# Row length of the involution stage's loads and stores: whole rows of 3136 to 6272 bytes, or runs of at most 896 bytes

## Chip, cores and metric

One core of one Trainium2 chip. The time is the device time of one execution in microseconds (us). A core has five engines that run their own instruction lists side by side: PE (TensorE, the matrix unit; its weight loads are listed apart as PEld), DVE (VectorE), ACT (ScalarE), POOL (GpSimd) and SP (SyncE, which here only issues DMA transfers). Sixteen DMA engines move data between the device memory (DRAM) and the on-chip memory, whose tiles have 128 partitions.

## The reference

A batch of 8 images of 256 channels, 56 x 56 pixels, float32, goes through two layers. `gn` is a group normalization over 32 groups, without scale and shift.

```python
# layer 0: involution, 16 groups of 16 channels, 7 x 7 neighbourhood
h = gn(x)
ker = einsum('bchw,oc->bohw', h, w_reduce) + b_reduce      # 256 -> 64 channels
ker = einsum('bchw,oc->bohw', ker, w_span) + b_span        # 64 -> 49 * 16
patches = the 49 shifted copies of h, zero outside the image
x = x + (ker * patches).sum(over the 49)                   # one kernel for the 16 channels of a group
# layer 1: residual block with ternary 3 x 3 convolutions
h = gn(x)
y1 = relu(batch_norm(tri_conv(h, w1)))
y2 = batch_norm(tri_conv(y1, w2))
x = x + relu(y1 + y2)
```

`tri_conv` quantizes its weights to -1, 0 and 1, convolves, and adds the product with the centre tap once more. `batch_norm` takes its mean and variance over the whole batch.

## The kernel before

The program has four stages, one after the other: the involution (layer 0), the first convolution, the second convolution, and a last pass that normalizes, adds and writes the output. The edited lines belong to the involution alone.

**Tiling of the involution.** The 256 channels are cut into 4 quarters of 64. A tile `x` of an image and a quarter (`xs[b, c]`) holds the 64 channels twice in its 128 partitions: the upper half of the image in the first 64, the lower half in the others, 28 x 56 = 1568 pixels (6272 bytes) in each partition. A half image is cut into patches of 3 x 8 pixels: 10 rows of patches (`ty`), 7 patches (`k`) in a row. With the border of a 7 x 7 neighbourhood a patch has 9 x 14 = 126 input pixels.

**The work for a row of patches.** The involution of a patch is a matrix product: the patch's 126 input pixels stand in the partitions of a tile `q`, and a generated matrix `a` maps them to the output pixels. `q` is a neighbourhood load (`load_q`, L726): 128 partitions of 7 patches x 128 channels, 896 floats or 3584 bytes each, from a copy of the image that lies ready in that order in DRAM. There are 8 images x 4 quarters x 10 rows = 320 of them. For each row:

- PE multiplies (`apply_row`, L839): 7 patches x 2 halves x 4 channel groups = 56 small matmuls into the accumulator tile `pa`;
- ACT and DVE take the result out (`pick_out`, L860: ACT at L867, DVE at L868), and POOL adds it to the image tile (L871);
- POOL adds the normalization's constants to a later `q` (`fill_rim`, L746, operation at L752), ACT writes the lower border (`fill_end`, L761).

**Beside it** PE generates the matrix `a` of the next quarter (`generate`, L804: products of the reduced image `kr` with the span weights `wl` into `pg`, taken to `a` by ACT at L827 and DVE at L831), reduces the next image (`reduce`, L700, products `pk`) and multiplies the kernel sums (`constant`, L774, products `ks`). DVE takes the statistics of the next image (`gn1_stats`), and quantizes the convolution weights in pieces (`quantize`, L277): a piece of 576 bytes a partition is loaded (L289), six planes are made, and they are stored in rows of 192 bytes (L318).

**Transfers and their order.** All of them go through SP's queue, in the order of the text. For each row of patches: a store of a finished image tile (`store_x1`, L891, rows 2 and 3 of the next quarter: 64 channels x 1568 floats, for the upper and the lower half) or half a tile of the next image (`load_x`, L599: 128 partitions x 784 floats, 3136 bytes), then one neighbourhood load (`prefetch`, L877), then the pieces of the quantization. SP waits at each until its buffer is free, and the ones after it wait behind it. There are 5 buffers for `q`, so the load for row n + 5 is issued when PE has read row n; POOL's rim addition for row n + 3 stands in row n (`surround`, `PLEAD = 2`). There are 7 buffers for `x`; a tile's buffer comes free when its two stores have landed.

**What fixes the order.** The text is recorded in order, and `pin` ties each engine's instructions to it; no scheduler moves anything. At the start SP issues the 8 halves of the first image, the weights `wf` for the first quantization, two tiles of span weights and biases (`sums`, L945 and L946), and the first five neighbourhood loads. The later stages load rows of 6496 bytes (`raw`), store rows of 6272 (`y1d`, `y2d`), and the last stage moves rows of 12,544.

Of the kernel before, what the change touches and what calls it, by code (L numbers as in the profile page):

```python
# [17 lines left out]
P = 128  # L18
# [10 lines left out]
CH = P // 2  # L29
# [6 lines left out]
PY, PX = 3, 8  # L36
# [4 lines left out]
QY, QX = PY + K - 1, PX + K - 1  # L41
# [6 lines left out]
HQ = TY * PY + K - 1  # L48
# [7 lines left out]
NQB = 5  # L56
PLEAD = 2
RIM_AT = 1

NCB = 4  # L60
NC = NHW // NCB
# [22 lines left out]
def involution_tri_block_kernel(  # L84
# [3 lines left out]
    nc = tc.nc  # L88
# [484 lines left out]
    with ExitStack() as ph1:  # L573
# [25 lines left out]
        def load_x(b, c, j):  # L599

            if j == 0:
                xs[b, c] = xpool.tile([P, NHW], F32, tag="x", name=f"x_{b}_{c}")
            part = slice(j * NHW // 2, (j + 1) * NHW // 2)
            nc.sync.dma_start(xs[b, c][:, part], x[b, c, :, part])

        def gn1_stats(b, c, j):

# [56 lines left out]
        prm, xs = {}, {}  # L664
        for c in range(NCQ):
            for j in range(2):
                load_x(0, c, j)
# [58 lines left out]
        def load_q(b, c, ty):  # L726

            q = qpool.tile([P, TX, P], F32, tag="q", name=f"q_{b}_{c}_{ty}")
            nc.sync.dma_start(q.rearrange("p k c -> p (k c)"),
                              x_nb[b, c, (HQ - QY - PY * ty) * QX:(HQ - QY - PY * ty) * QX + P, :])  # L730
            return q

        def rim_of(b, c):

            sides = work.tile([P, 2, P], F32, tag="sides", name=f"sides_{b}_{c}")
            tops = work.tile([P, 3, CH], F32, tag="tops", name=f"tops_{b}_{c}")
            rim = prm[b][3][:, c]
            for dst, k0, k1, f1 in ((sides, 0, 2, P), (tops, 2, 5, CH)):
                shape = [NQ, k1 - k0, f1]
                nc.gpsimd.tensor_tensor(dst[:NQ], rims_sb[:NQ, k0:k1].unsqueeze(2).to_broadcast(shape),  # L740
                                        rim[:NQ, :f1].unsqueeze(1).to_broadcast(shape), ALU.mult)
            low = work.tile([P, CH], F32, tag="low", name=f"low_{b}_{c}")
            nc.gpsimd.tensor_copy(low[:NQ], rim[:NQ, CH:])
            around[b, c] = sides, tops, low
# [132 lines left out]
        def prefetch():  # L877
            if queue:
                k = queue.pop(0)
                loads[k] = load_q(*k)  # L880
                bare.append(k)

        def surround(keep=PLEAD):
            for k in filled:
                fill_end(*k)
            filled.clear()
            while len(bare) > keep or bare and not queue:
                filled.append(bare.pop(0))
                fill_rim(*filled[-1])

        def store_x1(b, c, h):  # L891
            nc.sync.dma_start(
                x1_d[b][c // 2][c % 2 * CH:(c % 2 + 1) * CH, h * NHW:(h + 1) * NHW],
                xs[b, c][h * CH:(h + 1) * CH])

        gst = {}

# [91 lines left out]
        for m, (b, c) in enumerate(quarters):  # L989
# [6 lines left out]
            for ty in range(TY):  # L996
                r = c * TY + ty

                if last is not None and ty in (2, 3):
                    store_x1(*last, ty - 2)  # L1000
                elif more and r in X_AT:
                    load_x(b + 1, X_AT.index(r) // 2, X_AT.index(r) % 2)
                row = apply_row(b, c, a, ty)
                prefetch()

                if r == PARAMS_AT:
                    norm = params(b + 1) if more else gn2_params(0, b)
                next(norm, None)

                if ty == 1 and last is not None:  # L1010
                    gn2_stats(*last, TY)
                elif ty >= 2:
                    gn2_stats(b, c, ty - 1)
                if more and 4 <= r < 20:
                    gn1_stats(b + 1, (r - 4) // NCB, (r - 4) % NCB)
                pick_out(b, c, ty, *row)
                surround()
                if ty == RIM_AT and m + 1 < len(quarters):
                    rim_of(*quarters[m + 1])
                next(norm, None)  # L1020
                for _ in range(PER_ROW[ty]):
                    next(gen, None)
                if m * TY + ty >= QUANT_AT:
                    next(quant, None)
                pin()
# [6 lines left out]
        for h in range(2):  # L1032
            store_x1(*last, h)
# [46 lines left out]
    with ExitStack() as ph4:  # L1080
# [10 lines left out]
        for j in range(B * CT):  # L1091
            b, t = j // CT, j % CT
# [97 lines left out]
```

## Time and profile before

| what | value |
|---|---|
| median of 4 runs | 2215.27 us (2213.56 to 2220.21) |
| the profiled execution, device time | 2213.51 us |
| its span, first to last instruction | 2211.7 us |
| mean granted PE clock | 0.906 of full speed |
| involution, about 0 to 1090 us | PE busy 84% from 60 to 1085 us |
| two convolutions, 1100 to 1980 us | PE busy 98%, 440 us each |
| last pass, 1980 to 2212 us | DMA engines busy 99% |
| DMA packets in all | 156,252; 440.11 MB |
| neighbourhood load | 320 times 448 KB; issue on SP 0.33 us, landed after 4.2 us (medians) |
| image load | 64 times 392 KB; landed after 5.0 us |
| x1 store | 64 times 392 KB; landed after 5.5 us |

How to read the profile: *busy* is the time in which an engine had an instruction in work. A *wait* line names the waiting instruction, what released it, the sum of the idle time before it, how often, and the longest. "issue" there means that nothing the profile shows released it. The *DMA share* is the mean busy share of the sixteen DMA engines; queue q1 is the one that SP issues to, q8 carries packets of the kind "instruction". A DMA *packet* is one row of one transfer; each engine closes its part of a transfer with a packet of 4 bytes. The *granted clock* is the share of the full clock that PE was allowed. The *chain* of waits is followed back from the last instruction to what released each step.

### The profile page before, as it was taken

The page shows a single profiled execution, that of the slowest core. Times are in us where ns is not written, and L with a number is a line of the kernel's source. Part 1 is how long each engine was busy: PE and PEld are TensorE (multiplying, and loading weights), DVE is VectorE, ACT ScalarE, POOL GpSimd, SP SyncE. Part 2 cuts the span into 40 slices and gives each one's busy share as a digit, 9 for nine tenths or more (in the row PEclk, how much of TensorE's full clock was granted, in tenths as well). Part 3 has the DMA queues.
Part 4 walks back from the last instruction along what each step waited for, and adds up shares of the span by engine and source line. Part 5 has one row for each costly group of instructions (what it writes and reads, how often), then busy time and mean ns, then how long its engine had stood idle before and what let it go on. Part 6 is the DMA issues. An engine that isn't in the chain of part 4 may idle for free.

```text
span 2211.7 us, 71625 instructions
## 1 busy us (share of the span) xinstructions
PE 1756.4 (79%) x30192; PEld 1613.6 (73%) x30192; DVE 1731.5 (78%) x3257; ACT 1425.3 (64%) x3505; POOL 589.7 (27%) x965
## 2 busy tenths in 40 slices
PE   4888787988879788798599999997999999970000
PEld 3777676767767676677599999997999999970000
DVE  5768869677696867855599999998999999984444
ACT  3867677776767667677556666665566666663434
POOL 1546546564564646556500000000000000000000
PEclk9989899999999989899799999998999999985555
DMA  5558658575675757656643333335233333369999
GB/s 180 188 161 258 198 171 262 178 251 186 213 232 158 234 168 245 208 171 200 230 167 119 119 119 119 133 133 206 90 119 119 119 119 130 134 255 410 430 428 398
DMA packets 156252, 440.11 MB, mean 199 GB/s; under 512 B 63774, under 2 KB 74012, under 8 KB 148508
## 3 DMA queue, kind: packets, MB, share of 16 engines
q1 hardware_dynamic: 150336, 405.50, 53.0%
q10 hardware_dynamic: 5596, 30.03, 3.3%
q8 instruction: 239, 3.92, 0.7%
q14 instruction: 81, 0.66, 0.1%
HBM read 323.28 MB, written 112.20 MB: 197 GB/s over the span
## 4 chain that ended last, share of the span: by engine, by line
PE 63%; DMA 11%; DVE 9%; issue 8%; POOL 5%; ACT 3%; SPq 0%; ACTq 0%; POOLq 0%; DVEq 0%
PE c L516 39%; PE pg L823 11%; PE pa L854 7%; PE pk L711 4%; DMA y1f<-y1d 4%; POOL q L752 2%; ACT a L827 2%; DMA out_y<-x1f 2%; POOL x L871 2%; PE ks L787 1%; DMA x1f<-x1d 1%; DVE x1f L1103 1%; POOL x L801 1%; DMA y2f<-y2d 1%; DVE a L831 1%
## 5 line engine op out<-in xcount | busy, mean ns | idle before, releaser
L516 PE MATMUL c<-pl,wq 128*128 128x392 f32 x4608 | 857.4, 348 | 14.1 <-ACT pl L386 14.1
L516 PEld LDWEIGHTS c<-pl,wq 128*128 128x128 f32 x4608 | 855.5, 190 | 15.8 <-ACT pl L386 14.5
L827 ACT ACTIVATE a<-pg,bt 126x126 f32<-126x126 f32 (+1 forms) x2048 | 530.8, 456 | 112.4 <-PE pg L823 110.8
L823 PE MATMUL pg<-kr,wl 64*126 64x140 f32 (+1 forms) x6144 | 466.7, 297 | 59.3 <-issue 25.7
L823 PEld LDWEIGHTS pg<-kr,wl 64*126 64x126 f32 x6144 | 406.0, 199 | 85.4 <-issue 31.3
L854 PE MATMUL pa<-a,q 126*32 126x48 f32 x17920 | 288.9, 213 | 107.6 <-issue 83.7
L854 PEld LDWEIGHTS pa<-a,q 126*32 126x32 f32 x17920 | 237.3, 115 | 184.9 <-issue 113.4
L831 DVE TENSOR_TENSOR a<-pg,bt 126x504 f32<-126x504 f32 (+4 forms) x640 | 281.6, 482 | 53.4 <-PE pg L823 51.4
L868 DVE SCALAR_TENSOR_TENSOR inv<-pa,gn1s,inv 128x168 f32<-128x168 f32 x320 | 118.4, 370 | 220.2 <-ACT inv L867 219.0
L871 POOL TENSOR_TENSOR x<-x,inv 128x168 f32<-128x168 f32 x320 | 166.3, 520 | 461.8 <-DVE inv L868 399.4
L386 ACT CAST pl<-r 128x812 fp32r<-128x812 f32 x192 | 162.5, 868 | 143.2 <-DVE r L381 123.7
L366 POOL MEMSET xp<- 128x116 f32 x32 | 6.2, 195 | 825.6 <-DVE a L381 825.6
L752 POOL TENSOR_TENSOR q<-q,sides 126x256 f32<-126x256 f32 (+1 forms) x320 | 224.5, 702 | 4.2 <-DMA q<-in_x_nb 4.2
L387 DVE TENSOR_TENSOR pl<-r,pl 128x812 fp32r<-128x812 f32 x192 | 187.1, 1002 | 27.4 <-ACT pl L386 26.2
L451 ACT ACTIVATE dummy<-y,nc 128x1568 f32<-128x1568 f32 (+1 forms) x128 | 200.2, 1564 | 4.8 <-DVE y L536 3.5
L867 ACT ACTIVATE inv<-pa,gn1s 128x168 f32<-128x168 f32 x320 | 133.3, 417 | 102.2 <-PE pa L854 77.3
L143 DVE BATCH_NORM_STATS2 st<-x 128x6 f32<-128x392 f32 x256 | 138.0, 555 | 12.0 <-DMA x<-in_x 9.4
L801 POOL TENSOR_TENSOR x<-x,add 128x504 f32<-128x504 f32 (+1 forms) x128 | 126.7, 1021 | 12.2 <-ACT add L795 12.2
L1050 ACT ACTIVATE xp<-raw,gn 128x392 f32<-128x392 f32 (+1 forms) x124 | 82.5, 721 | 59.6 <-DVE a L381 58.8
L1070 ACT ACTIVATE xp<-raw,bi_bn,sc_bn 128x392 f32<-128x392 f32 (+1 forms) x124 | 82.3, 720 | 58.8 <-DVE a L381 57.1
L1101 DVE SCALAR_TENSOR_TENSOR y1f<-y2f,sc_bn,y1f 128x3136 f32<-128x3136 f32 (+2 forms) x20 | 56.6, 2831 | 63.9 <-DMA y2f<-y2d 50.1
L1103 DVE TENSOR_TENSOR x1f<-x1f,y1f 128x3136 f32<-128x3136 f32 (+2 forms) x20 | 55.3, 2772 | 50.9 <-DMA out_y<-x1f 31.5
(174 smaller groups left out, 1794.5 us busy)
## 6 DMA issues: line engine op xcount, KB each, us to landing
q<-in_x_nb SPq DMA_DIRECT2D x320, 448.0 KB, 4.2
raw<-x1d SPq DMA_DIRECT2D x32, 812.0 KB, 5.9
raw<-y1d SPq DMA_DIRECT2D x32, 812.0 KB, 5.8
x<-in_x SPq DMA_DIRECT2D x64, 392.0 KB, 5.0
x1d<-x SPq DMA_DIRECT2D x64, 392.0 KB, 5.5
y1d<-y SPq DMA_DIRECT2D x30, 784.0 KB, 3.3
y2d<-y SPq DMA_DIRECT2D x30, 784.0 KB, 3.3
y1f<-y1d SPq DMA_DIRECT2D x14, 1568.0 KB, 14.4
```

The source lines that it names most:

```text
L143: nc.vector.bn_stats(st[:, j, :], xt[:, j * NC:(j + 1) * NC])
L386: nc.scalar.copy(hi, r)
L387: nc.vector.tensor_tensor(lo, r, hi.bitcast(F32), ALU.subtract)
L451: nc.scalar.activation(dst, v, f, bias=shift[:, to:to + 1], accum_out=stats[:, to, j, n:n + 1])
L516: nc.tensor.matmul(ps[:, to, :NM], wq[k][:, t, dx, to * P:(to + 1) * P], part[:, t, :, dx:dx + W], start=(c == 0), stop=(c == last))
L752: nc.gpsimd.tensor_tensor(v, v, z, ALU.add)
L801: nc.gpsimd.tensor_tensor(x_, x_, v, ALU.add)
L823: nc.tensor.matmul(dst, wl[rows, c, gp, o:o + NQ], kr[py][rows, px, :], start=True, stop=True)
L827: nc.scalar.activation(dst[:, g + 1, p0 + j], ps[1][:NQ, j * nt + t0:j * nt + t1], AF.Identity, bias=bt[:, c, g + 1, p0 + j:p0 + j + 1])
L831: nc.vector.tensor_tensor(dst[:, g, p0:p0 + n].rearrange("q p t -> q t p"), ps[0][:NQ, t0 * n:t1 * n].rearrange("q (t p) -> q t p", p=n), ...
L854: nc.tensor.matmul(ps[o:o + 32, k * 2 * n:(k + 1) * 2 * n], q[:NQ, k, o:o + 32], av[:, t + k, g * 2 * n:(g + 1) * 2 * n], start=True, stop ...
L871: nc.gpsimd.tensor_tensor(xv, xv, iv.rearrange("p t (y x) -> p y t x", x=PX), ALU.add)
```

## The change

Three transfers of the involution are given a longest run: the image loads (`load_x`), the neighbourhood loads (`load_q`) and the stores of the involution's result (`store_x1`). The argument limits the last dimension of the transfer's access pattern, in bytes; the builder cuts a row into equal pieces that fit. The bytes moved, their places, the order of the instructions on every engine and all computation stay. A neighbourhood row of 3584 bytes becomes 4 runs of 896, an image row of 3136 bytes 4 runs of 784, a store's row of 6272 bytes 7 runs of 896.

```diff
 PLEAD = 2
 RIM_AT = 1
+RUN = 896
...
             part = slice(j * NHW // 2, (j + 1) * NHW // 2)
-            nc.sync.dma_start(xs[b, c][:, part], x[b, c, :, part])
+            nc.sync.dma_start(xs[b, c][:, part], x[b, c, :, part], max_dma_last_dim=RUN)
...
             q = qpool.tile([P, TX, P], F32, tag="q", name=f"q_{b}_{c}_{ty}")
             nc.sync.dma_start(q.rearrange("p k c -> p (k c)"),
-                              x_nb[b, c, (HQ - QY - PY * ty) * QX:(HQ - QY - PY * ty) * QX + P, :])
+                              x_nb[b, c, (HQ - QY - PY * ty) * QX:(HQ - QY - PY * ty) * QX + P, :],
+                              max_dma_last_dim=RUN)
             return q
...
         def store_x1(b, c, h):
             nc.sync.dma_start(
                 x1_d[b][c // 2][c % 2 * CH:(c % 2 + 1) * CH, h * NHW:(h + 1) * NHW],
-                xs[b, c][h * CH:(h + 1) * CH])
+                xs[b, c][h * CH:(h + 1) * CH], max_dma_last_dim=RUN)
```

## The prediction

> **What bounds the kernel now.** I read first the table of stretches, cut at the program's stages (columns: stretch, its length, busy time of PE, PE's weight loads, DVE, ACT and POOL with instruction counts, granted clock, mean busy share of the 16 DMA engines, GB/s).
>
> ```profile
> 60.00:1085.00 1025.00, 864.27 (x25044) 729.07 (x25040) 742.36 (x2041) 738.87 (x2619) 569.82 (x909) 0.93 0.66 206
> 1100.00:1540.00 440.00, 429.48 (x2308) 428.38 (x2308) 418.61 (x542) 279.81 (x379) 3.12 (x16) 0.98 0.37 138
> 1980.00:2211.70 231.70, 0.00 (x0) 0.00 (x0) 113.06 (x51) 91.11 (x39) 0.00 (x0) 0.50 0.99 416
> ```
>
> All three edited transfers run in the involution, the first row. There PE is busy 84% and every other engine less, the DMA engines 66%: PE sets the pace, with 161 us of idle. The convolutions are PE alone, the last stage is DMA alone, and neither issues an edited transfer. So the question is what the edit does to those 161 us and to the first 60. Second, the waits of PE in that stretch (us, times, longest):
>
> ```profile
> PE pa L854 <- issue: 76.5, 57, 3.8
> PE pg L823 <- issue: 25.7, 25, 3.2
> PE pg L823 <- DVE a L831: 21.1, 12, 3.4
> PE pa L854 <- ACT a L827: 13.0, 16, 1.7
> ```
>
> 102.2 us in 82 waits have no releaser among the instructions. Third, the DMA queues in the same stretch:
>
> ```profile
> q1 hardware_dynamic: 119181, 207.79, 64.7%
> q8 instruction: 198, 3.24, 1.3%
> q<-in_x_nb SPq DMA_DIRECT2D x315, 448.0 KB, 4.2
> ```
>
> q8 carries 198 packets of 16 KB, and PE ran 25,044 + 25,040 instructions: 253 for each packet, so I read q8 as PE's program, fetched over the same DMA engines; a packet took 0.013 x 16 x 1025 / 198 = 1.08 us. Fourth, one of the waits, in the timeline of PE:
>
> ```profile
> 242.21 0.74 PE L854 MATMUL pa<-a,q 126*32 126x48 f32 x49
> 246.72 0.38 PE L854 MATMUL pa<-a,q 126*32 126x48 f32 x7 [3.78 <-issue]
> ```
>
> PE stops after 49 of a row's 56 matmuls, all from one tile pair, so no data is awaited. The stretches around it:
>
> ```profile
> 242.90:244.30 1.40, 0.05 (x5) 0.00 (x0) 1.40 (x6) 1.39 (x6) 0.27 (x1) 1.00 1.02 355
> 244.30:245.20 0.90, 0.00 (x0) 0.00 (x0) 0.90 (x3) 0.00 (x0) 0.90 (x2) 1.00 0.99 346
> 245.20:246.70 1.50, 0.00 (x0) 0.00 (x0) 0.95 (x5) 0.00 (x0) 0.05 (x1) 0.58 0.42 107
> ```
>
> From 242.9 to 246.8 q8 has one packet, and a look at 244.20 to 244.35 holds its start. PE had run out 1.3 us before, while all engines worked on SP's data; the packet took about 1 us, and PE went on 1.5 us after it. So **the program fetch queues behind the data loads, and that is PE's largest idle in this stage.** In the convolutions PE has no issue wait: the DMA share is 0.37 and a fetch lasts over 20 us (37 in 885).
>
> **The change part by part.** The built program has the same instructions in the same order on all five engines; only shapes differ: a neighbourhood load of 128x896 words becomes 128x4x224, an image load 128x784 becomes 128x4x196, an x1 store 64x1568 becomes 64x7x224. So the limit is in bytes, and rows are 896, 784 and 896 bytes. Each of 16 engines had 8, 8 and 4 rows of a transfer and gets 32, 32 and 28: 24 more in each case.
>
> *Price of a row.* The last stage, on 12,544-byte rows above all, moves 422 GB/s, 26.4 bytes per ns and engine. The other end is a stretch that is nearly all 192-byte rows (the quantized weights' store), 1.2 us long:
>
> ```profile
> DMA packets 803, 0.18 MB, mean 147 GB/s; under 512 B 795, under 2 KB 795, under 8 KB 803
> q1 hardware_dynamic: 803, 0.18, 66.6%
> ```
>
> 0.666 x 16 x 1.2 = 12.8 us, less 8 rows of 3584 bytes at 0.136, leaves 11.7 us; over 768 rows (the other 27 small packets are 4-byte closings) that is 15 ns, of which 192 / 26.4 = 7.3 are the bytes: 7.7 ns of each row are fixed. 24 more rows: 0.185 us per transfer and engine. A neighbourhood load goes from 8 x 143.5 = 1.15 to 32 x 41.6 = 1.33 us (+16%). From 328.5 to 329.1 us, 128 rows of 576 bytes took 41.1% of 16 x 0.6 us, 30 ns each; the formula gives 29.5. The low bound is no fixed part, +0; the high one is the 12.8/803 = 16 ns of a whole small packet for each added row, 0.38 us. I take 0.185, the value that fits three sizes. The Trainium skill (DMA: Bandwidth & Descriptors, Specifications) puts line rate at 512 bytes and up, by which this edit would cost nothing on the engines; the 576-byte rows here run at 19 of 26.4 bytes per ns, so the row decides.
>
> The stretch from 60 to 1085 us has 315 neighbourhood loads, 55 image loads and 62 stores: 432 x 0.185 = 80 us more on every engine, and its share goes from 0.66 to 0.74.
>
> *The start.* Between 8 and 28 us the DMA share is 0.98 to 1.05, and the chain of waits goes through the load of the span weights, issued 13.8 and landed 24.7, behind eight image loads on SP's queue. Added: 8 x 0.185 = 1.5 us, bounds 0 and 3.0 (8 x 0.38). The neighbourhood loads there stand behind it.
>
> *Landing of the neighbourhood loads.* They land in 4.2 us (median); with 0.185 and one queued neighbour's 0.185 more it is 4.6. SP's issue also grows: 0.33 us now, 0.55 for the three-dimensional weight store, 0.2 more. Cover: a load is asked for two rows (2 x 1025/315 = 6.5 us) ahead of its rim addition on POOL, and that is about three rows ahead of PE's use. POOL waited for a load 6 times, 5.9 us in all. If all of those grow by 0.6 it is 4 us on POOL, which waits 392 us for DVE anyway; I put 2 us on the path (bounds 0 and 8). What is late next is SP: it stands for 573 us before neighbourhood loads until PE frees a buffer, 130 us before weight pieces until a weight store has landed, 16 us before image loads until an x1 store has. Each of these 55 landing waits grows by some 0.2 to 0.4 us and holds the neighbourhood load behind it, within the same two rows. Without that cover, 315 x 0.4 = 126 us.
>
> *The program fetch.* No row shows how its wait depends on row size, so it is bounded. Straight line: 102.2 us over 198 fetches is 0.52 us each at share 0.66, and none at 0.37: 1.8 us per unit of share, times 0.08, times 198: +28 us. Queue: with a wait that goes as share/(1 - share), 1.94 becomes 2.85 (x1.47): +48 us. High: the engine that carries the fetches has 198 x 1.08 / 1025 = 0.21 more, 0.87 becoming 0.95; the same law would triple its wait, but a PE that waits also asks for less, so I stop at a doubling, +102 us. Low: a fetch that only waits for a fixed number of accepted rows waits less, as each is 41.6 instead of 143.5 ns; half of the idle in that proportion, -36 us. I take +48: the wait shown above lasted ten row times of SP's queue after PE had stopped, nearest to a backlog, and the backlog grows.
>
> The same skill page (Queues, rings and completion order) says that a DMA engine goes round its queues packet by packet, some 9 to 17 descriptors each, at most 64. By that rule a fetch waits for one packet only: 17 rows of 41.6 ns, 0.7 us, instead of a load's 8 rows, 1.15 us, and 198 x 0.45 = 89 us at most would be gained; with whole loads of 32 rows as packets it is 198 x 0.18 = 36 us lost. It speaks against my sign; the wait above, of at least 1.3 us, is longer than one packet by either reading.
>
> **Sum.** The profiled execution took 2213.51 us (span 2211.7). 2213.5 + 1.5 + 2 + 48 = 2265. The median of the runs shown, 2215.3, is 1.8 above it: **2267 us**, +2.3%.
>
> **Rivals.**
> - *Faster: the fetch slips between small rows.* Place: q8 against SP's queue; it decides if the rows accepted ahead of a fetch are limited in number. For it: the row in service is 3.4 times shorter. Against: the convolutions' rows are nearly twice as long and their fetches stall nothing, and the wait shown was ten rows. 2213.5 + 3.5 - 36 + 1.8 = 2183.
> - *Hidden.* Fetches are as late as before and PE's cover takes the rest: 2213.5 + 3.5 + 1.8 = 2219 (+0.16%). For it: an average of 0.74 leaves 26% free. Against: the stalls come where the share is 1 already.
> - *The loads become the bound.* If rows in bursts cost more (a load alone from 138.1 to 139.9 us took 75% of 16 x 1.8 us, 167 ns a row, 1.2 of 0.14), the fetching engine's 0.95 passes 1: 1025 x 0.95 x 1.2 = 1169, +144: 2213.5 + 3.5 + 144 + 1.8 = 2363.
> - *The edit does nothing* if rows were counted in words; the built shapes exclude it.
>
> **How the numbers follow.** Forecast (2235 to 2335) 0.63; loads as bound 0.06; hidden 0.12; faster 0.19. Faster than by 0.2% (4.4 us, about what a measurement can tell): 0.19; within: 0.12; slower: 0.69. The range must take in the hidden case and part of the faster one: 2200 to 2335, with 0.12 below and 0.08 above; the high end is 2213.5 + 3 + 8 + 102 + 1.8 = 2328 and some clock loss (after the wait above the granted clock was 0.58).
>
> **What would show it.** Right: under 2 KB some 170,000 more packets, q1's share in the involution near 0.72, PE's issue waits near 150 us, POOL's waits for loads under 12 us, the convolutions and the last stage as long as now to 2 us. Wrong: issue waits below 102 us (the faster rival), or unchanged (hidden); POOL or PE waiting for loads for over 40 us (loads as bound); a row of 896 bytes that takes over 55 or under 36 ns.

## The result and the profile after

| | median | lowest to highest | runs |
|---|---|---|---|
| before | 2213.92 us | 2204.68 to 2235.29 | 72 |
| after | 2225.53 us | 2212.29 to 2236.01 | 48 |

After / before, compared within the groups of runs that shared a chip: **1.0043 [1.0032, 1.0053]**, some 9.5 us slower. The forecast was 2267 us with a range of 2200 to 2335: the direction holds and the time lies in the range, but the size is about five times too large.

The profiled execution after took 2213.71 us (span 2211.9), one of the shortest of its 48 and 0.2 us above the profiled one of before. Its rows therefore show what the edit changed, and hardly the 9.5 us. The table of stretches after, cut as before (length; busy time of PE, its weight loads, DVE, ACT, POOL; granted clock; DMA share; GB/s):

```profile
60.00:1085.00 1025.00, 864.21 (x24985) 726.74 (x24987) 743.79 (x2042) 739.69 (x2626) 569.62 (x907) 0.92 0.72 206
1100.00:1540.00 440.00, 429.01 (x2308) 427.91 (x2308) 419.03 (x542) 279.59 (x379) 3.13 (x17) 0.99 0.37 138
1980.00:2211.90 231.90, 0.00 (x0) 0.00 (x0) 113.06 (x51) 91.11 (x39) 0.00 (x0) 0.50 0.99 416
```

In the involution the DMA share has gone from 0.66 to 0.72 at the same 206 GB/s; PE was busy 864.27 us and is busy 864.21. The other stages are as they were. The DMA queues in that stretch, with packets, MB and share; and the loads' median time to landing:

```profile
DMA packets 284016, 211.15 MB, mean 206 GB/s; under 512 B 58257, under 2 KB 283633, under 8 KB 283761
q1 hardware_dynamic: 283761, 207.45, 70.6%
q8 instruction: 197, 3.23, 1.3%
q<-in_x_nb SPq DMA_DIRECT2D x313, 448.0 KB, 4.7
```

The same megabytes in 283,761 packets of SP's queue instead of 119,181, at a share of 70.6% instead of 64.7%. The waits of all engines there (us, times, longest), those of PE's and POOL's that matter:

```profile
PE pa L856 <- issue: 82.2, 59, 3.0
...
PE pg L825 <- DVE a L833: 23.2, 12, 3.4
...
PE pg L825 <- issue: 17.5, 17, 2.3
...
PE pa L856 <- ACT a L829: 12.2, 15, 1.7
...
POOL q L754 <- DMA q<-in_x_nb: 7.8, 7, 1.7
```

The two issue lines add up to 99.7 us in 76 waits; before they were 102.2 in 82. The wait that was to grow by 48 us has not grown, with the engines busier by 0.06. POOL waits for loads 7.8 us instead of 5.9. So the profile after has the cause that the prediction put first (a busier DMA) and not its effect.

### The profile page after: what moved, and what is told of

It is laid out like the page before. It is cut to its first block, busy times and chain, and to the rows that moved or that the text cites. A ratio compares the mean times of both kernels' runs of the same rounds, so it can differ in the third digit from the quotient of the medians.

```text
span 2211.9 us, 71625 instructions
## 1 busy us (share of the span) xinstructions
PE 1758.6 (80%) x30192; PEld 1613.5 (73%) x30192; DVE 1732.7 (78%) x3257; ACT 1425.7 (64%) x3505; POOL 590.3 (27%) x965
## 2 busy tenths in 40 slices
DMA packets 328284, 440.11 MB, mean 199 GB/s; under 512 B 63774, under 2 KB 299292, under 8 KB 320540
## 4 chain that ended last, share of the span: by engine, by line
PE 68%; DMA 10%; DVE 9%; issue 6%; ACT 4%; POOL 2%; ACTq 0%; SPq 0%; POOLq 0%; DVEq 0%
PE c L517 39%; PE pg L825 14%; PE pa L856 9%; PE pk L712 4%; DMA y1f<-y1d 4%; ACT a L829 3%; DMA out_y<-x1f 2%; PE ks L789 2%; DMA x1f<-x1d 1%; DVE x1f L1105 1%; DMA y2f<-y2d 1%; DVE a L833 1%; POOL q L754 1%; DMA wqd<-piece_w 1%; DVE st L144 1%
```

## The experiments

All are compared with runs of the kernel before on the same chip. Columns of the table: the ratio with its interval; then, from one profile each and from 60 us to the end of that kernel's involution, the DMA share, PE's issue waits, the lateness of the program fetch and PE's whole idle time. *Lateness* is worked out from the trace: on idle queues a packet of the program starts 1.12 us after PE has begun the 142nd instruction of a block of 256 (fitted to the trace: the earliest starts of the involution and of the convolutions lie 0.9 to 1.1 us after it alike); lateness is its start after that moment, as a mean over some 195 fetches. One mean has a standard error of about 0.11 us, so steps of 0.1 to 0.2 between two kernels are not read.

| kernel | ratio | share | issue us | lateness us | idle us |
|---|---|---|---|---|---|
| before, three profiles | 1 | 0.66 to 0.68 | 109, 111, 119 | 2.15, 2.21, 2.26 | 167, 172, 181 |
| after | 1.0043 [1.0032, 1.0053] | 0.72 | 105 | 2.14 | 165 |
| e1 after, once more | 1.0072 [1.0051, 1.0094] | 0.73 | 120 | 2.27 | 179 |
| e2 neighbourhood loads alone | 1.0030 [1.0009, 1.0051] | 0.71 | 117 | 2.26 | 171 |
| e3 image loads and stores alone | 1.0029 [1.0004, 1.0053] | 0.69 | 123 | 2.33 | 182 |
| e4 neighbourhood runs of 256 bytes | 1.0223 [1.0200, 1.0246] | 0.87 | 114 | 2.29 | 203 |
| e6 half of the loads, whole rows | 0.9815 [0.9773, 0.9856] | 0.50 | 51 | 1.59 | 137 |
| e7 half of the loads, 896 bytes | 0.9837 [0.9791, 0.9884] | 0.52 | 46 | 1.53 | 144 |
| e11 half of the loads, 256 bytes | 0.9844 [0.9812, 0.9876] | 0.60 | 55 | 1.59 | 151 |
| e13 runs of 1792 bytes, one transfer | 1.0007 [0.9985, 1.0029] | 0.68 | 118 | 2.22 | 176 |
| e12 the same rows, two transfers | 0.9931 [0.9906, 0.9956] | 0.69 | 93 | 2.03 | 161 |

The traces also show where a late fetch stops PE. With PE's instructions in the order of their starts, PE stands at one place of each block, 306 instructions after the one from which lateness is counted: 84 to 88 waits of over 0.3 us in the three profiles of before (128 to 143 us in all, counted from start to start), 84 (129 us) after. It goes on 1.4 us (median) after the packet has ended. PE takes 5.5 us (median) for these 306 instructions in the involution and 28.5 us in the convolutions. Less the 1.12 us, 1.0 us of the packet and the 1.4 us, a fetch can be some 2 us late in the involution before PE waits, and 25 us in the convolutions.

Nearly the whole difference in time lies in the involution: in all twenty profiles its first row of patches starts at 62.6 to 65.1 us, and what comes after its last row takes 1113 to 1116 us.

### The edit again, and its two parts

e1 is the changed kernel; e2 limits the runs of `load_q` alone, e3 those of `load_x` and `store_x1` alone. e5 and e15 are the kernel before, for a second and third profile.

> The changed kernel unchanged, for a second profile: the first profiled execution (span 2211.9 us) is among the shortest of 48 executions of this kernel (median 2225.5). Theory A, backlog: the program fetches wait longer behind a busier queue; a profile near the median shows issue waits of PE of 110 us or more from 60 to 1085 us (100 in the first one, 102 in the kernel before) and the rest as before. Theory B, offset: the busier queue and the shorter rows cancel at the fetch; issue waits stay at 95 to 107 us, and the 10 us come from the start (about 2 us) and from waits for landings in the other waits of PE, ACT and DVE. Ratio 1.003 to 1.006 in both.

> Only the neighbourhood loads in runs of 896 bytes: 315 of the 432 cut transfers of the steady part, none ahead of the span weights at the start. Theory A: the time goes with the added DMA work, 315 x 0.185 = 58 of 80 us, so some 6 of the 9.5 us, ratio 1.0025 to 1.0035. Theory B: little is left without the start and the image tiles, ratio 0.999 to 1.002. The start (first row of patches on PE) stands at 62.6 us as in the kernel before in both.

> Only the image loads and the x1 stores in short runs. The span weights land 1.5 us later and the first row starts 2.2 us later, as in the changed kernel. Theory A: 117 x 0.185 = 22 us more DMA work, with the start some 4 us in all, ratio 1.0015 to 1.0025. Theory B: 2 to 6 us, ratio 1.001 to 1.003. If the two parts do not add up to the whole (1.0043), the rest is an interaction.

> The kernel before, unchanged, for a second profile on the chip of the other kernels of this group. All theories: issue waits of PE between 60 us and the first convolution 105 to 125 us (109 in the first profile), q1's share 0.65, landing of the neighbourhood loads 4.2 us.

> The kernel before, for a profile on the chip of this group. All theories: issue waits 105 to 115 us, mean lateness of a fetch 2.1 to 2.25 us, POOL's waits for loads 4 to 12 us.

Measured: see the table; e5 took 2221.47 us and e15 2223.55 in one execution each. Each part alone costs about 0.3%, though by the prediction's price e2 adds 315 x 0.185 = 58 us of work to every DMA engine and e3 (55 + 62) x 0.185 = 22. e2's ratio is the one expected from the added work and e3's is above it, but the intervals are too wide to tell whether the loss follows that work. The issue waits of e1 to e3, 117 to 123 us, lie at the top of what three profiles of before show (109 to 119; the 119 of e15 is above the 105 to 115 expected) or just above it; nothing like 48 us is added. e3's profile is the slowest of its twelve executions. The intervals of e1 and of the first measurement of the same kernel just touch: groups of runs differ by some 0.2%, so differences of that size between groups are not read here.

### One suspected cost threefold: runs of 256 bytes

```diff
-RUN = 896
+RUN = 256        # load_q alone is limited
```

> Only the neighbourhood loads, in runs of 256 bytes: 14 for 1 row, 104 more per engine and load, 104 x 7.7 ns = 0.80 us, 252 us more DMA work from 60 to 1085 us; q1's share goes from 0.65 to about 0.87 (0.90 if a 256-byte row takes over 18 ns). Theory A: backlog doubles or more, issue waits of PE above 150 us, time up by 60 us or more (ratio above 1.025). Theory B: rows of 17 ns let a fetch in at once; issue waits at or below 100 us, ratio 0.99 to 1.01. Third theory, loads as the bound: landing above 6.5 us and POOL's waits for loads above 40 us, with issue waits unchanged.

The DMA queues and the waits of e4, 60 to 1145 us:

```profile
q1 hardware_dynamic: 643880, 210.13, 85.7%
q8 instruction: 199, 3.26, 1.3%
q<-in_x_nb SPq DMA_DIRECT2D x315, 448.0 KB, 5.5
```

```profile
PE pa L855 <- issue: 82.9, 67, 3.2
POOL q L753 <- DMA q<-in_x_nb: 78.7, 53, 3.7
...
PE pg L824 <- DVE a L832: 35.6, 20, 3.8
...
PE pg L824 <- issue: 30.9, 22, 3.5
```

At a share of 0.87 the issue waits are 113.8 us. The prediction's laws, put to this share, give 102 + 1.8 x 0.21 x 198 = 177 us (straight line) and 102 x (0.87 / 0.13) / 1.94 = 352 us (queue). **Both are refuted**: the fetch is hardly later with the engines a third busier. What does grow is POOL's wait for loads, from 7.7 us (60 to 1096 us) to 78.7 in 53 waits, though the loads land after 5.5 us where over 6.5 were expected for loads as the bound: it looks like a mild form of that rival, at rows of 256 bytes and not at 896 (e8 below tests it). The stretches of before and e4 to the end of the involution (columns as above):

```profile
60.00:1096.00 1036.00, 868.03 (x25232) 732.36 (x25228) 744.39 (x2047) 741.89 (x2625) 573.89 (x915) 0.93 0.66 208
60.00:1146.00 1086.00, 881.95 (x25232) 738.25 (x25234) 738.20 (x2048) 744.65 (x2629) 576.67 (x916) 0.91 0.87 197
```

Of the 50 us more, 36 are idle PE and 14 are longer busy time for the same instructions, with a granted clock of 0.91 for 0.93. (The other two profiles of before are 8 and 9 us longer, with 871 and 863 us of busy time.)

### Fewer loads, at three row lengths

Every second neighbourhood load is left out; the odd row of patches uses the tile of the even one.

```diff
-                loads[k] = load_q(*k)
+                loads[k] = loads[k[0], k[1], k[2] - 1] if k[2] % 2 else load_q(*k)
```

> Leaves out every second neighbourhood load: the odd row of patches works on the tile of the even row before it (the involution's result is another). Rows stay 3584 bytes; q1's share falls by about 0.17 to 0.49. Theory A (the backlog's share sets how late a program fetch starts, whatever the rows' length): issue waits of PE fall from 109 to some 40 to 60 us and the time by about 50 to 70 us. Theory C (the lateness does not depend on the share): issue waits stay above 90 us and the time falls by less than 20.

> The same, with the neighbourhood loads that are left in runs of 896 bytes: 158 x 0.185 = 29 us more DMA work on each engine, share up by 0.03. Theory A: issue waits of PE some 8 to 15 us above those of the kernel with whole rows, time likewise. Theory B (shorter rows let a fetch in sooner and cancel the higher share): issue waits equal within 5 us or lower, time within 5 us.

> Leaves out every second neighbourhood load (as in the earlier kernels of this kind; the result is another), the others in runs of 256 bytes: 158 x 0.80 = 126 us more DMA work than with whole rows, share about 0.61, near the 0.66 of the kernel before. Theory A (the share decides): issue waits of PE at 80 to 105 us (51 with whole rows at share 0.50, 110 at 0.66). Theory B (short rows let a fetch in): issue waits at 35 to 60 us.

PE's waits of e6, 60 to 1060 us:

```profile
PE pa L854 <- POOL q L752: 47.7, 42, 4.0
PE pa L854 <- issue: 32.1, 33, 2.6
PE pg L823 <- issue: 19.3, 18, 2.2
PE pg L823 <- DVE a L831: 17.7, 12, 3.4
```

The issue waits are less than half of before's, and a new wait of 47.7 us for POOL, which now adds the rim to a tile that PE has only just read, stands in the place of most of them; PE's whole idle is 137 us, 30 to 44 below before's. The time falls by 41 us, less than the 50 to 70 expected. The fetches are some 0.6 us earlier: take loads away, and the program comes sooner, as the prediction had it. But not by the *share*. e7 and e11 have the same number of loads in rows of a quarter and a fourteenth; the share climbs from 0.50 to 0.60, and lateness (1.59, 1.53, 1.59 us) and issue waits (51, 46, 55 us) stay. For e11, 80 us and more had been expected if the share decided. What counts here is how many loads there are, or how many bytes, and not how much time their rows take; which of the two, these runs don't separate.

### Is it a number of rows?

Short rows in the convolutions, where fetches are far apart and every late one can be looked at: raw loads in runs of 812 bytes and the stores of y1 and y2 in runs of 896 instead of 6496 and 6272, the involution as before.

```diff
-            nc.sync.dma_start(raw, src_d[b][t][:, r0 * W:(r0 + RAW) * W])
+            nc.sync.dma_start(raw, src_d[b][t][:, r0 * W:(r0 + RAW) * W], max_dma_last_dim=RUN)
```

> Involution as in the kernel before; the convolutions' loads of `raw` in runs of 812 bytes (8 for 1) and their stores of `y` in runs of 896 (7 for 1), all of them hidden behind PE. A convolution's fetches stall nothing, so the time stays (ratio 0.998 to 1.002); what is read is how late a fetch starts. In the two profiles of the kernel before, counted from the moment at which PE has started 142 of the last packet's 256 instructions, plus the 1.12 us of an idle queue, the 37 to 39 fetches of the convolutions start 1.6 to 1.9 us late on average, and up to 3 to 4.5 us inside a burst of four transfers. Theory A (a fetch waits for a time of backlog): the burst is 20% longer, lateness 1.6 us or more. Theory B (a fetch waits for a number of rows): a row goes from 240 to 40 ns, lateness falls below 1.0 us on average and below 1.5 us at the 90th percentile.

Ratio 1.0009 [0.9987, 1.0032]. Nine fetches of the convolutions wait in a burst of these transfers. Each outwaited 41 to 82 short rows of an engine (all that started while the fetch was late, over 16 engines) in 1.8 to 4.7 us, where the same nine fetches had outwaited 5 to 17 long ones in the kernel before, in 1.6 to 6.8 us; on average it is 3.0 us against 3.1. The mean lateness of all fetches from 1110 us to the end of the convolutions is 1.65 us, against 1.48 to 1.56 in the three profiles of before; below 1.0 was expected if a number of rows decided. A fetch doesn't wait for a fixed number of rows: it waits about as long however the data are cut. That refutes the faster rival as the prediction put it, and agrees with the changed kernel's fetches being no earlier either.

The Trainium skill (DMA: Bandwidth & Descriptors, Queues, rings and completion order) has an engine change queues after a packet of some 9 to 17 descriptors, at most 64. The 41 to 82 rows outwaited here are more than one such packet of 9 to 17; an engine's whole part of a transfer, 128 x 8 / 16 = 64 rows of a raw load or 128 x 7 / 16 = 56 of a store, taken as one packet within the page's limit, would fit better, though not the 82, which are more than one such part. No run here shows where an engine really changes over.

### The start, and the lead of the rim addition

e10 leaves the first image's loads whole and has the rest of the edit. `PLEAD` is the number of loads that stand issued without their rim addition. e14 is the kernel before with `PLEAD = 3`: a load has three rows instead of two before POOL needs it, and the rim addition comes one row later, nearer to PE's use. e8 is that with the 256-byte runs of e4.

> The changed kernel with whole rows for the first image alone, whose eight half tiles stand ahead of the span weights. All theories: the span weights land where they did in the kernel before (24.7 us), the first row of patches starts 1.5 to 2.2 us sooner than in the changed kernel, and that much of the loss goes: ratio 1.002 to 1.005.

> The kernel before with the rim addition one row later (PLEAD 3) and whole rows: the control for the 256-byte kernel with PLEAD 3 (ratio 1.0195; POOL's waits for loads gone, PE's waits for POOL's rim additions 53 us). If the late addition itself costs this: PE waits 40 us or more for POOL, ratio 1.010 to 1.020, and the landings were most of the 256-byte kernel's loss. If it costs nothing: PE's waits for POOL below 10 us, ratio 0.998 to 1.003, and the loss is the short rows' in another way.

> Neighbourhood loads in runs of 256 bytes as before (50 us slower than the kernel before, on another chip), with the rim addition one row later (PLEAD 3), so that a load has three rows instead of two before POOL needs it. If the 50 us are late landings: POOL's waits for loads fall from 79 to below 30 us and at least half of the loss goes (ratio at most 1.012). If they are the busy DMA engines or the program fetch: POOL's waits fall but the ratio stays above 1.017.

e10: 1.0045 [1.0022, 1.0067], lateness 2.22 us, issue waits 118. The span weights land at 24.70 us, as before the edit, where the edit has 26.19; a term of 1.5 us is below what the ratio tells.

e14: 1.0000 [0.9981, 1.0019], with other waits. Its lines, 60 to 1107 us:

```profile
PE pa L854 <- issue: 60.8, 54, 3.1
...
PE pa L854 <- POOL q L752: 36.0, 49, 3.4
...
PE pg L823 <- issue: 22.8, 22, 3.1
...
POOL q L752 <- DMA q<-in_x_nb: 2.3, 3, 1.3
```

The issue waits fall from some 113 to 83.6 us, and 36.0 us of waits for POOL appear; PE's idle is 168 us, within before's 167 to 181. Neither of the two expected cases came: PE waits for POOL almost as long as in the first, and the time is that of the second. A wait for POOL that falls between the request for a packet and its need gives the fetch more time; that the 30 us went this way is likely, and not shown. So **the sum of these waits is not the time they cost**: some 30 us of it can go and the time stays. The same holds for a part of what e6, e7 and e11 saved in issue waits, as their PE waits 48 to 50 us for POOL too; but their fetches, at 1.5 to 1.6 us, are well ahead of e14's 2.07, and that part is the loads'.

e8: 1.0195 [1.0146, 1.0245], against e4's 1.0223. Its lines, 60 to 1143 us:

```profile
PE pa L855 <- issue: 58.1, 52, 4.3
PE pa L855 <- POOL q L753: 52.6, 65, 3.4
...
POOL q L753 <- DMA q<-in_x_nb: 2.6, 2, 1.9
```

POOL's waits for loads are gone (2.6 us, from 78.7), PE waits 52.6 us for POOL instead, and PE's idle is 196 us. With e14 as control the lead itself costs nothing, so the reading that e4's loss is POOL waiting for landings is not confirmed. The loss is then the short rows' in another way, and in which stays open.

### The length of a transfer

If an engine ends its part of a transfer before it turns to the program, shorter transfers should help, whatever their rows. e12 makes two transfers of each neighbourhood load, each half the columns in rows of 1792 bytes; e13 has the same rows in one transfer, as control. A rival expected more transfers to do harm.

```diff
-            nc.sync.dma_start(q.rearrange("p k c -> p (k c)"),
-                              x_nb[b, c, (HQ - QY - PY * ty) * QX:(HQ - QY - PY * ty) * QX + P, :])
+            for j in range(2):
+                cols = slice(j * TX * P // 2, (j + 1) * TX * P // 2)
+                nc.sync.dma_start(
+                    q.rearrange("p k c -> p (k c)")[:, cols],
+                    x_nb[b, c, (HQ - QY - PY * ty) * QX:(HQ - QY - PY * ty) * QX + P, cols])
```

> Each neighbourhood load as two transfers of half the columns (128 partitions x 1792 bytes each): the same rows as one transfer in runs of 1792 bytes, twice the number of transfers. Theory D (how late a program fetch starts goes with the number of transfers in flight, not with the engines' time for a transfer): issue waits of PE at 130 to 200 us against 109 to 111 in the kernel before, mean lateness of a fetch at 2.6 us or more against 2.15 to 2.2, time up by 15 us or more (ratio above 1.007). Theory A (the share): 8 rows more per engine and load, 62 ns, 20 us of DMA work, share up by 0.02; issue waits within 10 us of the kernel before, ratio 1.000 to 1.003.

> The control: one transfer in runs of 1792 bytes, the same 8 more rows per engine and load. Theories A and D alike: issue waits 100 to 120 us, mean lateness 2.1 to 2.3 us, ratio 1.000 to 1.002.

On one chip: e13 1.0007 [0.9985, 1.0029], e12 **0.9931** [0.9906, 0.9956]. The rows are alike, the transfers half as long, and the kernel is faster than both the one before and the changed one. PE's waits, first e13 (60 to 1112 us), then e12 (60 to 1088 us):

```profile
PE pa L855 <- issue: 91.2, 61, 4.0
PE pg L824 <- issue: 26.5, 19, 4.1
PE pg L824 <- DVE a L832: 19.6, 13, 2.5
```

```profile
PE pa L857 <- issue: 76.0, 62, 3.8
PE pg L826 <- DVE a L834: 24.6, 13, 3.4
PE pg L826 <- issue: 16.5, 20, 1.9
```

117.7 us of issue waits become 92.5, while the number of waits stays (80 and 82): each is shorter. e13's profile is the slowest of its twelve executions, but the 92.5 lie below the 109 to 119 of before too. At the place in the program where a late fetch stops PE it is 85 waits and 138 us in e13, 86 and 116 in e12. The mean lateness falls from 2.22 to 2.03 us, hardly more than its error. Theory D, by which more transfers would do harm, is refuted at two a load; theory A did not foresee a gain.

Three more kernels test how far this goes: four transfers a load (e16, rows of 896 bytes), two for every edited transfer (e17), and two a load, each in runs of 896 bytes (e18).

> Each neighbourhood load as four transfers of 128 partitions x 896 bytes: the rows of the 896-byte kernel (q only, ratio 1.003), cut at transfer borders instead of inside one transfer. Theory E (a DMA engine finishes its part of a transfer before it turns to the program fetch, so the length of a part decides, 1.15 us whole, 0.6 in halves, 0.33 in quarters): issue waits of PE at 60 to 90 us, mean lateness below 2.0 us, ratio 0.985 to 0.995. Against it SP: 315 x 4 issues of 0.42 us are 530 us of its 1025; if SP becomes late, POOL's waits for loads exceed 30 us and the ratio is above 1. Theory A (the share of time): ratio 1.002 to 1.004 as with 896-byte runs.

> Neighbourhood loads, image loads and x1 stores each in two transfers of half the columns, whole bytes otherwise. Theory E: issue waits of PE below the 92 us of the kernel that halves the neighbourhood loads alone, ratio 0.988 to 0.993. Theory A: 0.9931 as without the two others, or above by 0.001.

> Neighbourhood loads in two transfers, each in runs of 896 bytes: 24 rows more per engine and load as in the changed kernel, parts of 16 rows and 0.67 us instead of 32 and 1.33. Theory E: most of the gain of the two transfers stays (0.9931 with 1792-byte rows), less some 0.002 for 16 rows more: ratio 0.993 to 0.998, issue waits 90 to 100 us. Theory A: ratio 1.002 to 1.004.

| | ratio | share | issue us | idle us | SP's waits in all, us | POOL for loads, us |
|---|---|---|---|---|---|---|
| e12 two | 0.9931 [0.9906, 0.9956] | 0.69 | 93 | 161 | 568 | 11 |
| e18 two, 896 bytes | 0.9951 [0.9930, 0.9973] | 0.73 | 103 | 165 | 547 | 29 |
| e17 all in two | 0.9941 [0.9915, 0.9967] | 0.70 | 85 | 165 | 503 | 28 |
| e16 four | 1.0250 [1.0211, 1.0289] | 0.74 | 83 | 199 | 243 | 97 |

e18 came as expected. e17 is no better than e12, a miss: fewer issue waits, more waits for loads. e16 was to gain by theory E and loses 2.5%. The waits that grow in it, with POOL's and then SP's view of e16 (60 to 1159 and 60 to 1090 us), and SP's view of e12 (60 to 1090 us) for comparison:

```profile
POOL q L755 <- DMA q<-in_x_nb: 96.7, 63, 4.2
...
PEld pa L857 <- POOL q L755: 35.6, 30, 3.1
...
PE pa L857 <- POOL q L755: 17.0, 13, 3.0
```

```profile
SPq L731 <- PE pa L857: 139.1, 49, 34.6
...
SPq L289 <- DMA wqd<-piece_w: 13.9, 22, 2.6
```

```profile
SPq L731 <- PE pa L857: 388.7, 178, 38.6
SPq L289 <- DMA wqd<-piece_w: 92.7, 50, 3.8
```

SP stands until PE frees a buffer for 573 us in the kernel before, for 389 with two transfers, for 139 with four. What fills its time instead is seen in the instructions that work on `q` (count: shortest/median/longest issue in ns, first and last start), of e12 and then of e16:

```profile
L731 SPq DMA_DIRECT2D q<-in_x_nb x630: 322/424/2411, 67.0 to 1078.4; - x158
```

```profile
L731 SPq DMA_DIRECT2D q<-in_x_nb x1171: 322/430/2100, 67.0 to 1089.6; - x196
```

1260 issues of 0.43 us are 542 us of SP's 1099; the loads land sooner after issue (3.3 us, from 4.0) and are late nonetheless, since SP gets to them late. So with four transfers **SP's issue** has become late, the case that was expected to bring POOL's waits above 30 us and the ratio above 1. That it makes the whole 2.5% is not shown. The stretches of e12 and e16:

```profile
60.00:1089.00 1029.00, 866.86 (x25242) 730.46 (x25238) 744.04 (x2048) 742.63 (x2630) 573.96 (x915) 0.93 0.69 209
60.00:1159.00 1099.00, 898.51 (x25208) 745.10 (x25212) 733.50 (x2047) 739.41 (x2629) 577.41 (x915) 0.90 0.74 194
```

Of the 70 us more, 38 are idle PE and 32 are longer busy time, with a granted clock of 0.90 for 0.93; and e8 has shown that POOL's waits for loads need not be the price. e16 says nothing against shorter transfers as such: its issue waits are 83 us, and its fetches are the least late of the kernels with all loads, about 1.65 us. Both fit theory E, but loads that are issued late may also stand less in a fetch's way.

That an engine ends its part first is not shown by this. e18's fetches are as late as before's (2.14 us), and its ratio is below 1 too. Shown is: two transfers of half the length are faster than one, by 0.76% at equal rows, with less of issue waits. Through which step the time comes back is open: between the profiles of e13 and e12 the stretch shortens by 23 us, 14 of them idle PE and 9 of them busy time.

The Trainium skill (DMA: Bandwidth & Descriptors, Rules for kernel authors) advises to coalesce many small transfers into one large one. Here 224 KB beat 448, and 112 KB lost, with the issuing queue late; the page's rule agrees with the second step only.

## Why the prediction was wrong in size

**What bounds the kernel: right.** PE sets the pace of the involution with the same busy time, and the other stages kept theirs (convolution 429.01 us of PE, 429.48 before).

**Packets and price of a row: right.** The whole execution has 328,284 packets where it had 156,252, 172,032 more (some 170,000 forecast), and q1's share in the involution is 70.6% where "near 0.72" was to be seen. A row of 896 bytes takes 41 ns in the median, 41.6 forecast; rows of 784 bytes 38, and those of 3584 140. The mean is 48.5 ns for the short and 174 for the long rows, as a part of either takes longer than the median: a load thus costs 32 x 48.5 - 8 x 174 = 160 ns more on its engine, where 185 were forecast, and the share rose to 0.72 and not to 0.74.

**The start: right at its place.** Before and after, the chain of waits from 8 to 64 us has this step (start, length, what):

```profile
13.83 10.86 DMA sums<-in_w_all
```

```profile
14.47 11.72 DMA sums<-in_w_all
```

The span weights land at 24.69 and 26.19 us: the 1.5 us of the sum (25.00 and 25.80 in the second profiles of the two). What of it reached the first row of patches can't be told: it starts at 64.8 us after and at 62.6, 64.2 and 64.0 us in three profiles of before.

**Landing: right.** 4.2 to 4.7 us (4.6 forecast), and POOL waits for loads 7.8 us, below the 12 that were allowed.

**The program fetch: the step that failed.** "With a wait that goes as share/(1 - share), 1.94 becomes 2.85 (x1.47): +48 us." It measured about 0: 99.7 us against 102.2 in the prediction's stretch, 105 and 120 against 109 to 119 to the end of the stage. The mechanism as far as the trace of before showed it (the fetch stands behind SP's loads) is supported by e6 in the lateness, 1.59 us for 2.15 to 2.26 with half of the loads. Wrong was to make the wait a function of the DMA *share*, and to take the rise of the share for a rise of the wait: e4 at 0.87 and e11 at 0.60 have the lateness of their whole-row partners. The three points that the prediction had (0.66 with waits, 0.37 without, and one wait of ten rows) differ in the number of loads and in the pace of PE's program too. The pace alone accounts for the point at 0.37: in the convolutions a fetch can be 25 us late before PE waits, and from 1110 us on none of before's is more than 7. And the one wait that chose +48 was not a common one: its fetch started 4.7 us late where the mean is 2.15. The bounds of -36 and +102 us held what came; the high one took all fetches to be carried by one engine, which no run here shows.

**The rule of packets that was weighed against the sign** would have had 89 us gained by packets of 17 rows or 36 lost by packets of a whole load. Neither came: the fetch waits about as long, for more rows.

**The rivals.** *Hidden* (2219 us, +0.16%) is nearest: fetches as late as before (2.14 us against 2.15 to 2.26) and unchanged issue waits are what it said. Its reason, the 26% that the engines stand free on average, does not carry it: at 13% free, in e4, the fetches are no later either. *The fetch slips between small rows* is refuted (e9, e11). *The loads become the bound* is not seen at 896 bytes (POOL's waits 7.8 us where over 40 were to be seen); at 256 bytes they are 78.7, and taking them away (e8) gave back little.

**What is left of 9.5 us.** Some 1.5 us stand at the start. The other 8 lie in the involution, as the rest of the program takes the same time in every profile, and are not located further. The direction was thus forecast right for a reason that did not hold: 48 of the 52 us forecast were a wait that did not grow. PE's idle from 60 us to the end of the involution is 167, 172 and 181 us in three profiles of before and 165 and 179 in two of after; PE's busy time 868, 871, 863 and 870, 870. The profiles of one kernel differ by more than is sought. The parts (0.30% and 0.29%) show that either kind of transfer costs something, and not where. The granted clock is a rival that no run separates: over whole executions its mean is 0.9005 in e1's six where the 23 of before on that chip have 0.9043, and 0.9004 in e10's against 0.9033. A lower clock may cost a part of the time, or only go with it.

## What to carry to other kernels

A wait that is put down to a busy resource is not yet a law of that resource's load: before a stall is scaled with a share, look for two points that differ in the share alone. When PE's waits have no releaser and a queue carries its program, see whether they stand at one place of each block of instructions, how much time the program gives a fetch before that place, and how many transfers the fetch stands behind; try the loads in two transfers, as far as the issuing queue has time to spare. And a sum of waits on PE is not time to be had: with the rim addition a row later 30 us of them turned into others and the time stayed.

## What the runs showed of the hardware

- The program of PE comes in 16 KB packets over the engines that carry the data. PE waits for a late one at one place, 306 instructions after the point from which its lateness is counted: 5.5 us of PE's time in the involution, 28.5 us in the convolutions.
- These packets start on average 2.1 to 2.3 us late beside 315 loads of 448 KB, and 1.5 to 1.6 beside half as many; the DMA share (0.66 to 0.87, and 0.50 to 0.60) made no difference to that.
- A row's fixed part is real and cost little time here: medians of 15, 18, 41, 74 and 140 ns for 192, 256, 896, 1792 and 3584 bytes. Four runs of 896 bytes take 17% more engine time than the row of 3584 by these medians, and with them in the neighbourhood loads the kernel took 0.3% longer; fourteen runs of 256 raised the share from 0.66 to 0.87, and the kernel took 2.2% longer.
- The same bytes in two transfers were faster than in one (0.9931 against 1.0007), and in four much slower (1.0250), with SP, which spends 0.43 us on each, late in issuing them.
